# Where the root mean squares of the last three batches are made in a three-stage fp32 kernel, and when its last rows are stored and its out-projection weights split

## The chip, the core and the metric

The kernel runs on one core of a Trainium2 chip. Its time is device microseconds of one execution on that core; the time before is the median of three runs. Five engines with queues of their own do the work: TensorE (PE in the profile, with its weight loads shown as PEld), VectorE (DVE), ScalarE (ACT), GpSimd (POOL) and SyncE (SP), which here only issues DMA transfers. An engine takes its instructions in order: one that waits holds everything behind it.

## The reference

Sixteen batches of 512 rows by 512 columns pass through three layers, all in fp32. The first is a cross attention with 16 heads over 77 context rows, with a residual sum and a layer norm. The second is a mamba block: a root mean square norm of the rows, an input projection to 2320 columns, a causal convolution of 4 taps, a gated state-space scan over 16 heads, a second root mean square norm and an output projection with a residual sum. The third is another cross attention. Cut to what matters here:

```python
# layer 0, its end: the rows x1 that the mamba block takes
resid = query + out
x = (resid - mu) * rsqrt(var + 1e-5) * gamma + beta
# mamba block
def _rms(x, w):
    return x * rsqrt(mean(x * x, axis=-1, keepdims=True) + 1e-5) * w
zxbcdt = _rms(x, norm_w) @ in_proj_w          # z, xBC, dt
dt = softplus(zxbcdt[..., -16:] + dt_bias)
xBC = silu(causal_conv(zxbcdt[..., 1024:2304]))
h = h * exp(dt * A) + (dt * xh) (x) B         # per step and head; y = h . C
u = _rms((y + D_skip * xh) * silu(z), gnorm_w)
x = x + u @ out_proj_w
# then layer 2: layer norm, cross attention, residual sum
```

The change concerns the number `rsqrt(mean(x*x) + eps)` of every row of `x1`, called r1 below.

## The kernel before

**Stages.** The kernel first makes the keys and values of both attentions (`phase_kv`), then runs `PhaseA` (first cross attention), `PhaseB` (mamba) and `PhaseC` (second cross attention), each as a software pipeline written out by hand. A product of fp32 matrices is made of three matmuls of split operands, a high part (name ending in `h`) and a low part (ending in `l`): `mm3` (L36 to L38) and `mm3_late` (L44 to L47). A split is a cast on ACT and a subtraction on POOL or DVE.

**Order.** PE, DVE, ACT and POOL run their instructions in the order of the Python code (`manual_schedule`). SP does so within the marked parts of the code, among them all units of the mamba stage; the loads that `open_out` issues stand outside of them.

**The end of PhaseA.** For each of the four row blocks m of a batch, `finish` (L483 to L489) adds the residual and takes mean and variance on DVE; after the fourth, the rows' reciprocal deviation is made (for the last batch in `rstd_split`: three DVE steps and twelve small POOL steps, the Newton steps of `newton`, L95 to L98). `norm` (L506 to L508) then scales a block on ACT and applies gamma and beta in two POOL passes. `store` (L514 to L516) writes the block to DRAM through SP and squares it on ACT into the unused tile `junk`, with the row sums kept in `ssq`. `rms`, `rms_step` and `store_rms` (L523 to L534) turn `ssq` into r1 and write it to DRAM: two small activations, five small POOL steps and a DMA. For the last two batches, 14 and 15, `ssq` is kept in SBUF (`g.ssq`) and r1 is made in the mamba stage by `last_rms` at unit 12 and stored by `store_last_rms` at unit 13.

**The seam.** `close_out` and `rest` of PhaseA run woven into the start of the mamba stage. `close_out` makes r1 of batches 12 and, in part, 13. After it come, in this order of the code, the four splits of batch 0's mamba input (`head_x`, tiles `nh` and `nl`, L942 and L943), its dt projection (`head_dt`, copy `dtr`, L953), a transpose on PE (`head_turn`), softplus on DVE (`head_steps`, which ends in `da`), and the projections of the B and C parts with their convolutions. `rest` is a generator of eight steps; units 0 and 1 of the mamba stage take one step at each of their four `next(side)` places. The steps finish, norm and store the rows of batches 14 and 15. What is left of it runs after unit 1.

**The mamba stage.** There are 128 units, eight for each batch; unit i is block (b, t) with b = i // 8 and t = i % 8 (the text calls t also k), and each block is two heads. In unit i three blocks are at work: `cur` = i is projected and convolved (`projx`, `convx`, `silux`, `projz`), `prev` = i - 1 gets its decay matrix on DVE (`decay`: two scans, L1075, and a product, L1077, on the tile `dbc`), its steps on ACT (`weigh`, tile `wu`; `steps`, tile `u`), its states (`states`, `st`) and its matmuls (`intra`, L1126, to `ps_y`; `inter`, L1133, to `ps_z`), and `prev2` = i - 2 is gated (`gate`: `yt` L1139 and `ebc` L1141 on DVE, then L1142 and L1143 on POOL) and split (`gate_split`: `gh`, squares `sq` or `sqa` on ACT, `gl` and a sum on POOL). SP issues in a unit the loads of two weight blocks (`wb`, L848), of `dbc` for the current block (L1036) and of `ebc` for the previous block (L1043). From unit 6 on, half an output projection of an earlier block runs in each unit (`out_half`); `tail_norm`, `tail_pre` and `tail_end` finish a batch's output rows in the units k = 2 to 5 of the next batch.

**The next batch's input.** Beside this, units k = 0 to 5 bring batch b + 1 into shape. At k = 0 `load_x1` loads its rows to `XN` (`xn`, four DMAs, L902) and its r1 to `RS` (four DMAs, L903). `prepare` is called at one place of the units k = 1 to 5, after `intra`: at k = 1 row blocks 0 and 1 are scaled by r1 on ACT (`scale_x1`, L908); at k = 2 blocks 2 and 3 are scaled and blocks 0 and 1 turned on DVE (`turn_x1`, L126); at k = 3 blocks 2 and 3 are turned; at k = 4 the turned rows are stored (`x1t`, L919), at k = 5 loaded again (`xf`, L925).

**The out-projection weights.** `open_out` returns a generator of eight splits. Each scales a slice `xr` by the gate norm's weight (ACT, L170), casts the high part (ACT, L171), subtracts the low part (`wopl`, POOL, L172) and has SP load the slice three further on into the same buffers (L165). Units 3 to 9 take one of them each, unit 4 two, at the first `next(side)` of the unit, which stands after `convx` and before `steps`.

Of the kernel before, what the change touches and what calls it, by code (L numbers as in the profile page):

```python
# [8 lines left out]
F32 = mybir.dt.float32  # L9
FR = mybir.dt.float32r  # L10
U8 = mybir.dt.uint8
AF = mybir.ActivationFunctionType
# [280 lines left out]


class PhaseA:

# [183 lines left out]
    def finish(self, b, m):  # L480
# [9 lines left out]
        if m == KT - 1:  # L490
            rs = self.rstd(b, mv[:, :, 1], "a")
            nb_ = neg_mean(g, self.pf, mv[:, :, 0], rs, [P, KT], "nb")
            late = b - (g.nb - 2)
            self.MV[b] = (rs, nb_, g.ssq[:, late, :] if late >= 0 else self.pf.tile([P, KT], F32, name="ssq"))
            self.NP = [(b, k) for k in range(KT)]
# [14 lines left out]
    def store(self, b, m):  # L510
        g, nc = self.g, self.nc
        ssq = self.MV[b][2]
        xb = self.XB.pop((b, m))
        nc.sync.dma_start(g.x1[b][m * P:(m + 1) * P, :], xb)  # L514
        junk = self.pf.tile([P, D], F32, name="junk", bufs=1)
        nc.scalar.activation(junk, xb, AF.Square, accum_out=ssq[:, m:m + 1])  # L516
# [138 lines left out]
    def close_out(self):  # L655
# [7 lines left out]
        while self.SQ:  # L663
            self.store_next()
        self.rms(x - 1)

    def rest(self):
# [10 lines left out]
        self.norm_next()  # L678
        self.store_next()
        yield  # L680
        self.norm_next()
        self.store_next()
        yield
        for _ in range(4):
            self.store_next()
            self.norm_next()
            yield
        self.store_next()
        self.store_next()

# [60 lines left out]
class PhaseB:  # L751


    def __init__(self, g):
        self.g, self.nc = g, g.nc
        self.n = 8 * g.nb
        self.drain = False
# [16 lines left out]
    def open_out(self):  # L774
# [19 lines left out]
        return splits()  # L794

    def last_rms(self):

        y = rstd_split(self.g, self.p2, self.g.ssq.rearrange("p b k -> p (b k)"), [P, 2 * KT], "q", 1.0 / D)
        self.r_last = y.rearrange("p (b k) -> p b k", b=2)

    def store_last_rms(self):
        for j in range(2):
            self.nc.sync.dma_start(self.g.r1[self.g.nb - 2 + j], self.r_last[:, j, :])

# [90 lines left out]
    def load_x1(self, b):  # L895
# [3 lines left out]
        src = self.g.x1[b].rearrange("(a m r) d -> a r m d", m=KT, r=32)  # L899
        rs = self.g.r1[b].rearrange("(m r) a -> a r m", r=32)  # L900
        for a in range(4):
            self.nc.sync.dma_start(self.XN[32 * a:32 * a + 32], src[a])  # L902
            self.nc.sync.dma_start(self.RS[32 * a:32 * a + 32], rs[a])  # L903

# [22 lines left out]
    def prepare(self, b, step):  # L927

        if step in (1, 2):
            self.scale_x1((0, 1) if step == 1 else (2, 3))  # L930
        if step in (2, 3):
# [261 lines left out]
    def unit(self, i, side=iter(())):  # L1193
# [356 lines left out]
def tile_kernel(ctx: ExitStack, tc, ins, out, phases="kabc", dbg=None):  # L1550
# [27 lines left out]
    g.eps = cst.tile([P, 1], F32, name="eps")  # L1578
    g.ssq = cst.tile([P, 2, KT], F32, name="ssq") if "a" in phases else None
# [3 lines left out]
    A, B, C = PhaseA(g) if "a" in phases else None, PhaseB(g), PhaseC(g)  # L1583

# [32 lines left out]
    if "b" in phases:  # L1617
        B.open_main()
        with tc.manual_schedule(engines={E.SP}):
# [110 lines left out]
```

## Time and profile before

| | |
|---|---|
| median of 3 runs | 2948.78 us (2946.47 to 2951.47) |
| the profiled execution | 2947.86 us, of which 2946.1 us are the span from the first to the last instruction |
| PE busy | 2865.4 us (97%) |
| DVE, ACT, POOL busy | 2369.4 (80%), 1824.1 (62%), 1491.4 us (51%) |
| mean granted clock of PE | 0.986 |
| PE busy up to 660 us (keys, values, first attention) | 648.81 of 660.00 us |
| PE busy from 660 to 735 us | 64.23 of 75.00 us |
| PE busy from 735 to 2370 us (mamba) | 1607.87 of 1635.00 us |
| PE busy from 2370 to 2946 us (second attention) | 544.51 of 576.00 us |

A line of the timeline reads: start and length in us, engine, line of the kernel, operation, output and inputs by the program's tile names, shapes, count, and in brackets the idle time of that engine just before and what ended it. Tiles of several buffers share one name. "SPq" rows are DMA issues; their length is what SP spends on them, waiting included. A busy share is an average over stages with different limits, so what a part is worth has to be read in its own stretch of time.

### The profile page before, as it was taken

Reading aid. Unit: us, or ns where it says so; the run is one execution under the profiler, and the core shown is the slowest. Engines: PE = TensorE matmul, PEld = TensorE weight load, DVE = VectorE, ACT = ScalarE, POOL = GpSimd, SP = SyncE. Lnnn points to the kernel's source line nnn. Section 1 sums busy time; section 2 is a strip of 40 time slices with the busy share of each in tenths; the row PEclk is TensorE's granted clock in tenths of the full one; section 3 lists DMA queues with packets and bytes.
Section 4 is the critical chain, followed back from the end, with each engine's and each line's share of the span. In section 5 each row is a group of like instructions: output and inputs, shape, how many; then the busy total and the mean of one; then the engine's idle time right before and its main releaser. Section 6 shows DMA issues by size and latency. Waiting matters only on the chain.

```text
span 2946.1 us, 47590 instructions
## 1 busy us (share of the span) xinstructions
PE 2865.4 (97%) x15712; PEld 2151.8 (73%) x15712; DVE 2369.4 (80%) x3781; ACT 1824.1 (62%) x4972; POOL 1491.4 (51%) x1201
## 2 busy tenths in 40 slices
PE   9999999998899999999999999999999978999999
PEld 7755555555677888788788878878887866777776
DVE  4277777777688998998899899889989978777764
ACT  3256666665666566666666666666666547666663
POOL 1036776766756555555555555555555533333331
PEclk9999999999899999999999999999999988999999
DMA  7345665555656665665666566566656567898974
GB/s 234 95 124 157 179 180 158 162 154 170 206 181 205 206 203 183 208 215 183 203 206 207 183 207 213 183 202 206 208 186 199 170 203 214 267 270 268 272 237 147
DMA packets 421604, 578.22 MB, mean 196 GB/s; under 512 B 105982, under 2 KB 248494, under 8 KB 421358
## 3 DMA queue, kind: packets, MB, share of 16 engines
q1 hardware_dynamic: 421358, 575.18, 63.0%
q8 instruction: 125, 2.05, 0.3%
q14 instruction: 121, 0.99, 0.1%
HBM read 445.10 MB, written 129.42 MB: 195 GB/s over the span
## 4 chain that ended last, share of the span: by engine, by line
PE 69%; DVE 24%; DMA 2%; ACT 2%; issue 1%; POOL 1%; SPq 0%; DVEq 0%; ACTq 0%; POOLq 0%
PE ps_o L36 7%; PE ps_o L38 6%; PE ps_o L37 6%; PE ps_w L44 5%; PE ps_w L45 5%; PE ps_w L47 5%; DVE dbc L1075 5%; DVE acc L869 4%; DVE dbc L1077 3%; PE ps_z L1133 3%; PE ps_y L1126 2%; PE ps_y L36 2%; PE ps_s L390 2%; PE ps_z L1477 2%; PE ps_w L1433 2%; PE ps_x L417 2%
## 5 line engine op out<-in xcount | busy, mean ns | idle before, releaser
L44 PE MATMUL ps_w<-nh,wb 128*128 128x512 f32 x1092 | 454.3, 416 | 0.0
L45 PE MATMUL ps_w<-nh,wb 128*128 128x512 f32 x1092 | 430.0, 394 | 0.0
L1142 POOL TENSOR_TENSOR yt<-yt,ebc 128x384 f32<-128x384 f32 x128 | 224.1, 1751 | 396.6 <-DVE ebc L1141 396.6
L1075 DVE TENSOR_TENSOR_SCAN dbc<-dbc,delta 128x512 f32<-128x512 f32 x256 | 387.2, 1555 | 0.0
L869 DVE SCALAR_TENSOR_TENSOR acc<-ps_w,cw,acc 128x511 f32<-128x511 f32 (+2 forms) x384 | 286.1, 745 | 27.4 <-ACT acc L867 18.3
L47 PE MATMUL ps_w<-nl,wb 128*128 128x512 f32 x1092 | 293.6, 391 | 0.0
L1077 DVE TENSOR_TENSOR dbc<-dbc,gm 128x1024 f32<-128x1024 f32 x128 | 270.1, 2110 | 5.5
L1149 POOL TENSOR_TENSOR gl<-yt,gh 128x512 fp32r<-128x512 f32 x128 | 169.7, 1326 | 200.3 <-ACT gh L1148 200.2
L1143 POOL TENSOR_TENSOR yt<-yt,sz 128x512 f32<-128x512 f32 x128 | 253.9, 1984 | 10.0
L47 PEld LDWEIGHTS ps_w<-nl,wb 128*128 128x128 f32 x1092 | 205.3, 188 | 44.5
L44 PEld LDWEIGHTS ps_w<-nh,wb 128*128 128x128 f32 x1092 | 207.3, 190 | 38.5 <-issue 2.4
L45 PEld LDWEIGHTS ps_w<-nh,wb 128*128 128x128 f32 x1092 | 207.5, 190 | 35.9
L1449 POOL TENSOR_TENSOR sc<-sc,sm 128x616 f32<-128x616 f32 x64 | 78.7, 1230 | 298.3 <-DVE sm L1448 255.6
L1103 ACT ACTIVATE u<-ps_x,dt 128x64 f32<-128x64 f32 x1024 | 222.8, 333 | 0.0
L392 DVE TENSOR_TENSOR sc<-ps_s,mt 77x2048 f32<-77x2048 f32 x64 | 146.1, 2283 | 94.0 <-PE ps_s L390 93.9
L1094 ACT ACTIVATE wu<-ps_x,et 128x64 f32<-128x64 f32 x768 | 171.8, 326 | 59.8 <-PE ps_x L1085 59.8
L867 ACT ACTIVATE acc<-ps_w,cb,cw 128x512 f32<-128x512 f32 x128 | 99.8, 780 | 172.2 <-PE ps_w L47 172.2
L38 PE MATMUL ps_o<-woph,gl 128*128 128x512 f32 x496 | 196.4, 396 | 0.0
L37 PE MATMUL ps_o<-wopl,gh 128*128 128x512 f32 x496 | 196.1, 395 | 0.0
L36 PE MATMUL ps_o<-woph,gh 128*128 128x512 f32 x496 | 195.9, 395 | 0.0
L1444 ACT ACTIVATE sc<-sc,mx 128x77 f32<-128x77 f32 x512 | 176.9, 354 | 0.2 <-DVE mx L1437 0.2
L1058 ACT ACTIVATE xs<-acc 128x512 f32<-128x512 f32 x128 | 81.2, 635 | 134.2 <-DVE acc L869 128.1
(348 smaller groups left out, 7510.4 us busy)
## 6 DMA issues: line engine op xcount, KB each, us to landing
wb<-win SPq DMA_DIRECT2D x288, 512.0 KB
dbc<-dec SPq DMA_DIRECT2D x128, 512.0 KB
ebc<-ecs SPq DMA_DIRECT2D x256, 96.0 KB
pt<-pb SPq DMA_DIRECT2D x62, 384.0 KB
xt<-in_xT_dram SPq DMA_DIRECT2D x64, 256.0 KB
xb<-in_x_dram SPq DMA_DIRECT2D x64, 256.0 KB
x<-xb SPq DMA_DIRECT2D x64, 256.0 KB
xf<-x1t SPq DMA_DIRECT2D x16, 1024.0 KB
```

The lines of the kernel that those rows point to most:

```text
L36: nc.tensor.matmul(ps, ah, bh, start=start, stop=False)
L37: nc.tensor.matmul(ps, ah, bl, start=False, stop=False)
L38: nc.tensor.matmul(ps, al, bh, start=False, stop=stop)
L44: nc.tensor.matmul(ps, ah, bh, start=k == 0, stop=False)
L45: nc.tensor.matmul(ps, al, bh, start=False, stop=False)
L47: nc.tensor.matmul(ps, ah, bl, start=False, stop=k == len(rhs) - 1)
L869: nc.vector.scalar_tensor_tensor(acc[:, s:], ps[:, :S - s], cw[:, j, 3 - s:4 - s], acc[:, s:], op0=ALU.mult, op1=ALU.add)
L1075: nc.vector.tensor_tensor_scan(flat, flat, self.delta.rearrange("p c i -> p (c i)"), 0.0, op0=ALU.mult, op1=ALU.add)
L1077: nc.vector.tensor_mul(lm, lm, o.gm[:, None, :, :].to_broadcast((P, 2, 4, P)))
L1103: nc.scalar.activation(w.u[:, c, h, :], w.pu[:, f:f + 64], AF.Copy, scale=o.dtc[:, c, 2 * t + h:2 * t + h + 1])
L1142: nc.gpsimd.tensor_add(yt[:, P:], yt[:, P:], t2)
L1143: nc.gpsimd.tensor_mul(yt, yt, w.sz)
```

## The change

For the last three batches (13, 14 and 15, `own_rms`), PhaseA no longer squares the rows it stores, and neither `rms` for batch 13 nor the step at units 12 and 13 for batches 14 and 15 is there any more. The mamba stage makes r1 of these batches from the rows that it has loaded: `prepare` squares all four row blocks at k = 1 (`rms_x1`, into the tile `sq` that `gate_split` uses too) and makes r1 with `rstd_split`; at k = 2 it scales all four blocks. Their r1 is neither stored nor loaded. In `rest`, the stores come later and in groups: two at step 4, two at step 7, four after the last step, where there was one a step from step 3 to step 8 and two after it. The norms stay where they were. A unit's weight split moves from the first `next(side)` to the third, behind `load_ecs` and `head_bt` and before `intra`; the second split of unit 4 moves from the second to the fourth.

```diff
+def own_rms(g, b):
+    return b >= max(g.nb - 3, 1)
 class PhaseA:
     def finish(self, b, m):
...
-            late = b - (g.nb - 2)
-            self.MV[b] = (rs, nb_, g.ssq[:, late, :] if late >= 0 else self.pf.tile([P, KT], F32, name="ssq"))
+            self.MV[b] = (rs, nb_, None if own_rms(g, b) else self.pf.tile([P, KT], F32, name="ssq"))
     def store(self, b, m):
...
         nc.sync.dma_start(g.x1[b][m * P:(m + 1) * P, :], xb)
+        if ssq is None:
+            return
         junk = self.pf.tile([P, D], F32, name="junk", bufs=1)
         nc.scalar.activation(junk, xb, AF.Square, accum_out=ssq[:, m:m + 1])
     def close_out(self):
...
         while self.SQ:
             self.store_next()
-        self.rms(x - 1)
     def rest(self):
...
         self.finish(y, 3)
         self.norm_next()
-        self.store_next()
         yield
         self.norm_next()
         self.store_next()
+        self.store_next()
         yield
-        for _ in range(4):
+        for k in range(4):
+            self.norm_next()
+            if k == 2:
+                self.store_next()
+                self.store_next()
+            yield
+        while self.SQ:
             self.store_next()
-            self.norm_next()
-            yield
-        self.store_next()
-        self.store_next()
 class PhaseB:
-    def last_rms(self): ...
-    def store_last_rms(self): ...
     def load_x1(self, b):
...
+        self.own = self.own_rms and own_rms(self.g, b)
         for a in range(4):
             self.nc.sync.dma_start(self.XN[32 * a:32 * a + 32], src[a])
-            self.nc.sync.dma_start(self.RS[32 * a:32 * a + 32], rs[a])
+            if not self.own:
+                self.nc.sync.dma_start(self.RS[32 * a:32 * a + 32], rs[a])
+    def rms_x1(self):
+        g, nc = self.g, self.nc
+        ssq = self.p2.tile([P, KT], F32, name="ssq", bufs=1)
+        for m in range(KT):
+            junk = self.p2.tile([P, S], F32, name="sq", bufs=1)
+            nc.scalar.activation(junk, self.XN[:, m, :], AF.Square, accum_out=ssq[:, m:m + 1])
+        self.RS = rstd_split(g, self.p2, ssq, [P, KT], "q", 1.0 / D)
     def prepare(self, b, step):
-        if step in (1, 2):
-            self.scale_x1((0, 1) if step == 1 else (2, 3))
+        if step == 1 and self.own:
+            self.rms_x1()
+        elif step in (1, 2):
+            self.scale_x1(range(4) if self.own else (0, 1) if step == 1 else (2, 3))
     def unit(self, i, side=iter(())):
...
-        if self.g.ssq is not None and i == 12:
-            self.last_rms()
-        if self.g.ssq is not None and i == 13:
-            self.store_last_rms()
 def tile_kernel(ctx: ExitStack, tc, ins, out, phases="kabc", dbg=None):
...
             B.head_dt(0)
             if A:
-                A.rms_step(y - 2)
-                A.store_rms(y - 2)
                 A.project(y, 1)
                 A.finish(y - 1, 3)
...
-                B.unit(i, islice(wo, 0 if i < 3 or i > 9 else 1 + (i == 4)))
+                B.unit(i, chain((None, None), islice(wo, 0 if i < 3 or i > 9 else 1 + (i == 4))))
```

More of the change, by code (lines that the diff above doesn't have):

```diff
@@ L751, with __init__ @@
 class PhaseB:
-    def __init__(self, g):
+    def __init__(self, g, own):
         self.g, self.nc = g, g.nc
+        self.own_rms = own
         self.n = 8 * g.nb
@@ L794, in open_out @@
         return splits()
[L796 to L803, printed above, removed]
     def setup(self):
@@ L1578, in tile_kernel @@
     g.eps = cst.tile([P, 1], F32, name="eps")
-    g.ssq = cst.tile([P, 2, KT], F32, name="ssq") if "a" in phases else None
     E = mybir.EngineType
@@ L1582, in tile_kernel @@
     nc.scalar.preload_act_table_set("natural_log_exp_and_others")
-    A, B, C = PhaseA(g) if "a" in phases else None, PhaseB(g), PhaseC(g)
+    A, B, C = PhaseA(g) if "a" in phases else None, PhaseB(g, "a" in phases), PhaseC(g)
     def consts():
```

## The prediction

> **What bounds the kernel now.** I read the page's engine rows first, then ten-microsecond windows around the seam between the cross-attention stage and the mamba stage, then the timeline of each engine there, and last the timeline of one settled mamba batch.
>
> ```profile
> PE 2865.4 (97%) x15712; PEld 2151.8 (73%) x15712; DVE 2369.4 (80%) x3781; ACT 1824.1 (62%) x4972; POOL 1491.4 (51%) x1201
> ```
>
> ```profile
> 730.00:740.00 10.00, 3.57 (x23) 2.70 (x21) 2.17 (x6) 5.23 (x17) 9.17 (x15) 0.78 0.27 97
> 740.00:750.00 10.00, 5.01 (x21) 4.08 (x20) 7.53 (x6) 4.87 (x11) 9.76 (x6) 0.84 0.33 124
> ...
> 770.00:780.00 10.00, 7.79 (x52) 6.35 (x51) 8.44 (x9) 7.50 (x23) 6.56 (x5) 1.00 0.45 172
> 780.00:790.00 10.00, 9.44 (x39) 7.88 (x37) 5.71 (x10) 4.55 (x12) 6.20 (x5) 0.66 0.86 235
> ```
>
> PE is 97% busy, so only the other 3% or work on its path can move the end. The window rows give length, then busy time of PE, PEld, DVE, ACT and POOL, then granted clock, DMA share and GB/s. At the seam (730 to 830) PE is idle for 22.8 us; in the rows above it is busy for 3.57, 5.01, 7.79 and 9.44 us of 10, and the clock falls to 0.66. Who holds PE there:
>
> ```profile
> 734.77 0.63 ACT L516 ACTIVATE junk<-xb 128x512 f32<-128x512 f32 x1 [6.65 <-POOL xb L508]
> 739.92 10.65 SPq L514 DMA_DIRECT2D x<-xb  x4
> 767.83 0.33 SPq L165 DMA_DIRECT2D xr<-in_L_out_proj_w_dram  x1
> 768.69 1.09 SPq L1043 DMA_DIRECT2D ebc<-ecs  x2
> 773.00 0.56 DVE L1141 TENSOR_TENSOR ebc<-ps_z,ebc 128x384 f32<-128x384 f32 x1 [1.50 <-DMA ebc<-ecs]
> 786.63 0.56 DVE L1141 TENSOR_TENSOR ebc<-ps_z,ebc 128x384 f32<-128x384 f32 x1 [4.25 <-DMA ebc<-ecs]
> 798.78 0.56 DVE L1141 TENSOR_TENSOR ebc<-ps_z,ebc 128x384 f32<-128x384 f32 x1 [2.76 <-DMA ebc<-ecs]
> 811.65 0.56 DVE L1141 TENSOR_TENSOR ebc<-ps_z,ebc 128x384 f32<-128x384 f32 x1 [3.47 <-DMA ebc<-ecs]
> ```
>
> Two queues block at their head. ACT's squares of the last rows (L516) wait for POOL's norm of those rows (L508). SP's reload of `xr` (L165) waits until POOL's split at 765.54 (2.26 us) has read the old one, and the `ebc` load of the same unit stands behind it; DVE then waits 1.50, 4.25, 2.76 and 3.47 us for it.
>
> In a settled batch (one lasts 103 us) the chain lies on PE, but from unit k=2 to k=4 on DVE without a gap:
>
> ```profile
> 1987.69 0.60 ACT L1068 ACTIVATE sz<-ps_w 128x512 f32<-128x512 f32 x1 [0.68 <-PE ps_w L47]
> 1988.18 1.32 ACT L908 ACTIVATE xn<-xn,r 128x512 f32<-128x512 f32 x2
> 1988.82 0.75 DVE L1139 SCALAR_TENSOR_TENSOR yt<-xs,dsk,ps_y 128x512 f32<-128x512 f32 x1 [1.77 <-PE ps_y L1126]
> 1990.06 3.11 DVE L1075 TENSOR_TENSOR_SCAN dbc<-dbc,delta 128x512 f32<-128x512 f32 x2
> 2001.27 1.30 DVE L126 STREAM_TRANSPOSE xb<-xn 128x512 f32<-128x512 f32 x2
> ```
>
> From 1988.82 DVE is never idle until 2045.8, and at 2023.4 PE itself waits about 0.5 us for DVE's states. What delays DVE at 1988.82 comes out at the end one for one. That is where the change puts its new work.
>
> **What it takes away at the seam.** Durations are of one profiled execution: 2946.1 us of span, 2947.86 in all, 0.92 below the median 2948.78.
>
> Twelve squares with their reads leave ACT (0.61 us each by the steps 723.70, 724.31), with their waits on POOL. For batch 13, the squares at 696.33 and 698.95 and the two small activations at 699.71 go; now they hold ACT's four casts `nh` at 700.15 and the copy `dtr` at 702.22. PE waits 1.54 us for that copy and 0.68 us for `da` after it, 2.2 us together. The copy can then follow its matmul (697.26, 1.06 us). DVE's softplus, now from 705.77, can start 3.9 us sooner, though POOL's `nl` lies beside it and may stretch it by 1 to 2 us. The next limit is the projection of (0,0), 2.2 us sooner, and its bias on ACT, so DVE's conv moves from 718.15 to about 715.1, and POOL's Newton steps for batch 15 from 725.80 to about 722.8. I take 2.5 us, with 0 and 3.1 as ends.
>
> From there POOL's chain stays: twelve Newton steps, then the norms of six row blocks, up to 750.2. It only moves with its start, to 747.7. The last four stores still stand in SP in front of unit 2's loads (the 10.65 us row), so putting stores later doesn't free SP by itself; it lets the first `ebc` load (738.22 now) go 13 us sooner. ACT's steps `u` (736.10) come by 733 and PE runs ahead, but the gate of (0,1) needs its `ebc`, issued behind those stores. It lands at 758.4 in place of 760.93. The idle time that the squares cost (5.70 and 6.43 us on PE) mostly turns into a wait for this load; I count 2.5 us and no more.
>
> **The weight splits later.** Each is two ACT steps (0.71, 0.62), one POOL subtraction (2.26, beside DVE's scans) and one SP load. It moves past ACT's `u`, `st`, `gh`, `xs` and `sz`, past POOL's `gl` and `sqa` adds, and past SP's weight and `ebc` loads of the unit. So `ebc` of a unit goes out right after the load before it, 5 to 14 us ahead of its use. Behind the waiting `xr` load stand now the row stores `x1t` of unit 4, `xf` of unit 5 and the next unit's `dbc`. The out-projection first needs splits 0 to 3 in unit 6 and 4 to 7 in unit 10; both come in time.
>
> What is next is DVE's own work: `yt` 0.66, `ebc` 0.47, scans 3.14, product 2.05, conv 2.25, states 0.77, together 9.34 us a unit (1.2 more in unit 3 for two turns); PE needs 8.6. The scans of (0,2) to (0,6) start now at 761.41, 773.47, 787.11, 799.26 and 812.13. I expect 758.9; 769.5 (10.6 later); 778.9 (9.4 later); then, since `dbc` and `ebc` stand behind two `xr` loads of unit 4 that wait for POOL until about 781, 790.3; then PE decides with the first half out-projection in unit 6: from the states at 787.1, 0.87 + 0.44 + 2.8 + 2.8 + 0.67 + 2.8 + 1.02 + 0.87 = 12.3, and 0.47 for `ebc`, 799.9. That is 12.2 us sooner than 812.13, and nothing after that depends on the seam. Ends: 7 if the start brings nothing and the late `dbc` isn't absorbed (9.7 - 2.5); 15 if all four `ebc` waits go (12.0) with 3.1 of start.
>
> **What it adds, three times.** In unit k=1 of batches 12, 13 and 14, ACT's two scalings are replaced by four squares. They start at 1988.4 (the scratch `sq` is free when POOL's add of 1987.06, 1.30 us, is done); 4 x 0.61 plus the last read is 1991.0. Three small DVE steps (0.2 each, as `q` below) wait for them, and behind those in DVE's order stands the gate of unit k=2: `yt` goes from 1988.82 to 1991.6, +2.75. ACT itself has room: its next `wu` is wanted at 1995.4. POOL then does twelve Newton steps. The trace has that sequence once, in the part that the change removes:
>
> ```profile
> 892.31 0.16 DVE L106 TENSOR_SCALAR q_ve<-ssq 128x8 f32<-128x8 f32 x1
> 894.58 2.33 DVE L1075 TENSOR_TENSOR_SCAN dbc<-dbc,delta 128x512 f32<-128x512 f32 x2
> 896.94 1.22 DVE L1077 TENSOR_TENSOR dbc<-dbc,gm 128x1024 f32<-128x1024 f32 x1
> 892.97 0.20 POOL L95 TENSOR_TENSOR q_t<-q_y 128x8 f32<-128x8 f32 x1 [1.83 <-DVE q_y L109]
> 899.04 1.02 POOL L1142 TENSOR_TENSOR yt<-yt,ebc 128x384 f32<-128x384 f32 x1
> ```
>
> While POOL does small steps in place of its 128x384 and 128x512 ones, DVE's scans take 2.33 in place of 3.11 and the product 1.22 in place of 2.13: from `yt` to conv 4.63 us, not 6.43. So DVE gets 1.8 back and is 0.95 late. But POOL's gate is late: from the first Newton step to its end took 8.46 us, so from 1991.65 to 2000.1; ACT's `gh` (1996.40 now) follows at 2000.4, then `sqa`, `xs`, `sz`, and only then the scalings, all four now in unit k=2. The first is done at 2003.2, the second at 2003.8. DVE's turns would start at 2002.2, and wait: `yt` of unit k=3 starts at 2005.1, not 2003.12. That is 2.0 us a batch, 6.0 in all. Low end 0.95 (no wait of the turns), 2.9 in all. High end 2.75 + 1.0 without the faster scans, and the clock.
>
> On the clock: PE's idle 2.21 us before 779.02 was followed by half-speed matmuls (0.63 in place of 0.39 each), 2.4 us lost up to 787.7. My stalls in a late batch come in pieces of 0.5 and 1.5 us, and pieces of 1.37 and 0.89 us (before 792.63 and 795.03) left the clock at 1.00; so I add nothing, and 2.4 a batch at the high end, (2.75 + 1.0 + 2.4) x 3 = 18.5. [...]
>
> The rest costs nothing I can find: twelve `r1` loads (0.43 us of SP each) and three `r1` stores go, from stretches where SP waits anyway; the old last-rows step ran when DVE had just left the chain (PE's from 891.40).
>
> **The sum.** 2947.86 - 12.2 + 6.0 = 2941.7; against the median, 2942.6, 0.21% faster. A measurement of this kernel can tell about 0.2%, 5.9 us, from no change.
>
> **Rivals.** *Cheap batches*: the turns don't wait, 2.9 in place of 6.0 (for it: the once-seen sequence; against it: POOL's 8.46 us are measured): 2939.5, down to 2936 with 15 us of gain. Chance 0.15. *The block moves on*: SP's wait for `xr` now holds `x1t`, `xf` and `dbc`, and the seam gives only 7: 2947.6; for it that all loads share one queue, against it that `dbc` has a unit of lead. Chance 0.23. *Slower*: DVE's wait for the squares at k=1 with full scans and the clock loss behind it. It decides from 12.2 / 3 = 4.1 us a batch; at 6.15 it gives 2948.78 - 12.2 + 18.5 = 2955. For it: DVE has no gap from k=2 to k=4; against it: the scan of 2.33. Chance 0.12. The forecast, 2939.5 to 2946.5, keeps 0.50.
>
> Faster by over 0.2% (below 2942.9): 0.15 and some 0.31 of the forecast, 0.46. Within: the rest of the forecast and the moved block, 0.42. Slower: 0.12. The range 2936 to 2951 leaves out the slower case and little more.
>
> **What would show it.** Right: no ACT wait on POOL's `xb` at the seam; DVE's `ebc` waits gone from unit 3 on but one of several us at about 758; scans there 9 to 11 us apart; in the three late batches a DVE wait for ACT of about 4 us before the small steps, scans of 2.33, turns waiting for ACT about 1 us, and batches of about 105 us. Wrong: late batches of 103 or over 107, or `ebc` waits at 780 to 812 as before.

## The result and the profile after

The changed kernel takes 2957.03 us (median of 8 runs, 2952.98 to 2961.79), the kernel before 2950.32 (8 runs, 2946.47 to 2952.21). The ratio is 1.0023, with a 95% interval of 1.0013 to 1.0032: slower by 0.23%, where the prediction had 0.21% faster and a range that ended at 2951. The profiled execution of the changed kernel took 2961.79 us (span 2960.0), 4.8 above its median; that of before took 2947.86, 2.5 below its own. So the profiles overstate the difference, and where a time is compared below, it is a median; where a place is compared, it is an offset inside a trace.

The first row of the page, busy time by engine, shows no engine with more work:

```profile
PE 2866.9 (97%) x15712; PEld 2149.2 (73%) x15712; DVE 2372.1 (80%) x3787; ACT 1820.4 (61%) x4970; POOL 1494.9 (51%) x1220
```

The windows of the seam in the changed kernel (length; busy time of PE, PEld, DVE, ACT, POOL; granted clock, DMA share, GB/s):

```profile
730.00:740.00 10.00, 7.38 (x46) 6.20 (x47) 6.01 (x9) 8.89 (x26) 9.47 (x11) 1.00 0.31 110
740.00:750.00 10.00, 4.96 (x34) 3.54 (x32) 7.62 (x12) 1.73 (x9) 9.76 (x7) 0.94 0.21 79
750.00:760.00 10.00, 6.79 (x23) 5.70 (x24) 0.00 (x0) 5.22 (x13) 2.64 (x3) 0.55 0.98 304
760.00:770.00 10.00, 4.58 (x29) 3.52 (x27) 7.66 (x7) 3.09 (x12) 6.32 (x4) 0.80 0.43 156
...
790.00:800.00 10.00, 8.67 (x56) 7.02 (x51) 3.01 (x8) 7.43 (x22) 5.38 (x5) 1.00 0.92 258
800.00:810.00 10.00, 4.48 (x29) 3.67 (x29) 7.33 (x7) 1.61 (x4) 6.00 (x4) 0.84 0.93 319
```

PE is better off from 730 to 740 (7.38 us busy, 3.57 before), as forecast. Then two new holes stand where DVE does nothing: all of 750 to 760, and most of 790 to 800. From 730 to 830 PE is busy for 75.05 us; before it was 77.17. The timeline of the engines in the changed kernel names the holes:

```profile
733.68 15.83 SPq L518 DMA_DIRECT2D x<-xb  x6
751.48 0.62 ACT L1160 CAST gh<-yt 128x512 fp32r<-128x512 f32 x1 [9.75 <-POOL yt L1155]
753.06 1.09 SPq L1055 DMA_DIRECT2D ebc<-ecs  x2
762.24 0.56 DVE L1153 TENSOR_TENSOR ebc<-ps_z,ebc 128x384 f32<-128x384 f32 x1 [14.51 <-DMA ebc<-ecs]
783.92 4.42 POOL L172 TENSOR_TENSOR wopl<-xr,woph 128x512 fp32r<-128x512 f32 x2 [2.42 <-ACT woph L171]
786.20 0.34 SPq L165 DMA_DIRECT2D xr<-in_L_out_proj_w_dram  x1
786.64 3.55 SPq L929 DMA_DIRECT2D x1t<-xb  x4
790.29 1.28 SPq L165 DMA_DIRECT2D xr<-in_L_out_proj_w_dram  x1
793.78 1.24 SPq L1055 DMA_DIRECT2D ebc<-ecs  x2
802.56 0.56 DVE L1153 TENSOR_TENSOR ebc<-ps_z,ebc 128x384 f32<-128x384 f32 x1 [9.48 <-DMA ebc<-ecs]
```

Of the four waits of before, those for `ebc` of (0,2), (0,3) and (0,5) (1.50, 4.25 and 3.47 us) are gone or below 0.7 us, as forecast. But there is one of 14.51 us for the load of (0,1), which is issued behind the last six stores and lands 8.1 us after that, and the one for (0,4) has grown from 2.76 to 9.48 us: SP stands at unit 4's first `xr` reload until POOL has done the split, then issues four `x1t` stores, the second `xr`, weights and `dbc`, and only then `ebc`.

A late batch (the first, batch 12, from the end of unit k=1):

```profile
1990.58 0.63 ACT L912 ACTIVATE sq<-xn 128x512 f32<-128x512 f32 x1
1993.60 0.17 DVE L106 TENSOR_SCALAR q_ve<-ssq 128x4 f32<-128x4 f32 x1 [4.39 <-ACT sq L912]
1994.09 0.75 DVE L1151 SCALAR_TENSOR_TENSOR yt<-xs,dsk,ps_y 128x512 f32<-128x512 f32 x1
1995.22 2.33 DVE L1087 TENSOR_TENSOR_SCAN dbc<-dbc,delta 128x512 f32<-128x512 f32 x2
1997.58 1.22 DVE L1089 TENSOR_TENSOR dbc<-dbc,gm 128x1024 f32<-128x1024 f32 x1
2001.90 0.71 DVE L66 TENSOR_SCALAR g_y<-g_ve 128x4 int32<-128x4 int32 x1
2002.62 0.62 ACT L1160 CAST gh<-yt 128x512 fp32r<-128x512 f32 x1 [3.92 <-POOL yt L1155]
2003.44 1.16 DVE L71 SCALAR_TENSOR_TENSOR g_t<-g_y 128x4 f32<-128x4 f32 x1
2004.67 2.55 ACT L918 ACTIVATE xn<-xn,q_y 128x512 f32<-128x512 f32 x4
2006.29 1.30 DVE L126 STREAM_TRANSPOSE xb<-xn 128x512 f32<-128x512 f32 x2
```

The wait of DVE for the squares (4.39 us), the fast scans (2.33) and the product (1.22) are there as told. New are small steps of `tail_norm` that take 0.71 and 1.16 us. Before, the same two took 0.17 and 0.16 us:

```profile
1998.43 0.17 DVE L66 TENSOR_SCALAR g_y<-g_ve 128x4 int32<-128x4 int32 x1
1999.42 0.16 DVE L71 SCALAR_TENSOR_TENSOR g_t<-g_y 128x4 f32<-128x4 f32 x1
```

**A ruler.** Whole runs of the changed kernel lie up to 8.8 us apart. Inside a trace, the start of DVE's product with `gm` in each of the 128 units is far steadier: from batch 2 to batch 11 its offset against before moves by 0.6 us at most (e12_lead, which changes these batches, apart). I use these offsets for every kernel; (b,t) is the product of tile t of batch b. For the seam, the kernel's offset at the last scores of the first attention (near 670 us in all) is taken off. Columns: `dtv` of batch 0 (a tile of DVE's softplus, the start of the seam), then units, then what the three late batches add each, and the rest of the program after the mamba stage (this one from spans given to 0.1 us; all in us against before, minus is earlier):

```
kernel              dtv   (0,1)  (0,2)  (0,4)  (0,5)  (1,1) | a late batch       | after it
after             -1.56   -4.73   2.81  -1.45   5.26   3.17 | 2.81  2.77  2.92   |  3.16
splits moved only  0.59    0.56   1.08  -3.88   2.65   0.63 | none               | -0.37
splits not moved  -4.01   -7.09  -0.88  -0.60  -0.34  -0.34 | 2.80  2.78  2.88   |  0.76
ebc early         -3.63   -6.71  -6.98 -11.70  -9.60 -10.89 | 2.80  2.83  2.87   |  3.49
4 raw buffers     -1.54   -4.74   1.39  -3.54  -3.50  -5.90 | 2.83  2.77  2.91   |  0.76
before, ebc early -0.06   -1.35  -1.86  -6.87  -8.36 -10.61 | none               | -3.61
```

The seam of the changed kernel, at unit (1,1), is 3.17 us later than before in its own profile; three later kernels with the same seam code had 1.37, -2.12 and 1.13. Their mean is 0.9, where the forecast had -12.2. A late batch costs 2.8 to 2.9 us in every trace that has the change's order of steps.

### The profile page after: what moved, and what is told of

It reads as the page before. It is cut to its first block, busy times and chain, and to the rows that moved or that the text cites. A ratio compares the mean times of both kernels' runs of the same rounds, so it can differ in the third digit from the quotient of the medians.

```text
span 2960.0 us, 47593 instructions
## 1 busy us (share of the span) xinstructions
PE 2866.9 (97%) x15712; PEld 2149.2 (73%) x15712; DVE 2372.1 (80%) x3787; ACT 1820.4 (61%) x4970; POOL 1494.9 (51%) x1220
## 4 chain that ended last, share of the span: by engine, by line
PE 69%; DVE 24%; DMA 2%; ACT 2%; issue 2%; POOL 2%; SPq 0%; DVEq 0%; ACTq 0%; POOLq 0%
PE ps_o L36 7%; PE ps_o L38 6%; PE ps_o L37 6%; PE ps_w L44 5%; PE ps_w L45 5%; PE ps_w L47 5%; DVE dbc L1087 4%; DVE acc L868 4%; DVE dbc L1089 3%; PE ps_z L1145 3%; PE ps_y L1138 2%; PE ps_y L36 2%; PE ps_s L395 2%; PE ps_z L1485 2%; PE ps_w L1441 2%; PE ps_x L422 2%
## 5 line engine op out<-in xcount | busy, mean ns | idle before, releaser
L38 PE MATMUL ps_o<-woph,gl 128*128 128x512 f32 x496 | 196.0, 395 | 0.0
```

The lines of the kernel that those rows point to most:

```text
L38: nc.tensor.matmul(ps, al, bh, start=False, stop=stop)
```

## The experiments

Theory Q: the seam's gain was made and then eaten by two `ebc` loads that stand behind a blocked head of SP's queue, and a late batch costs what DVE waits for the squares. Its rivals are named in each expectation. Each ratio is to runs of the kernel before on the same chip in the same session; the interval is 95%.

### The parts: e2_rows and e1_splits

The changed kernel with the splits back at their old place:

```diff
-B.unit(i, chain((None, None), islice(wo, 0 if i < 3 or i > 9 else 1 + (i == 4))))
+B.unit(i, islice(wo, 0 if i < 3 or i > 9 else 1 + (i == 4)))
```

> The changed kernel with the weight splits back at the first and second place of the unit: the other two parts of the change alone. Theory Q: the late batches cost 2.8 us each as in the changed kernel (8.5 in all); at the seam the start is 1 us earlier and the waits of before for ebc (4.25, 2.76, 3.47 us) come back, so that (1,1) stands -2 to +1 us against before; total 2957 to 2960. Rival S: the late batches are as dear, but the seam alone is worse than before by over 2 us (the last six stores held back too long), total 2961 or more. Rival P: without the split move (1,1) stands at -3 or better, total 2952 to 2955.

2956.96 us, ratio 1.0022 (1.0012 to 1.0032). The late batches cost 2.80, 2.78 and 2.88. At the seam `ebc` of (0,1) is waited for by 13.18 us, and the waits of before come back as 1.99, 4.08, 3.02 and 2.98; (1,1) is at -0.34. As theory Q had it: rows and stores without the splits bring nothing at the seam either. (The expectations of e1_splits, e2_rows and e3_ecs count (1,1) with the attention's offset left in: so counted it is -0.06, -3.96 and -14.50. For e2_rows that is rival P's figure, but 3.6 us of it were there before the seam began, and the total lies at Q's 2957 and not in P's 2952 to 2955.)

The kernel before, with the opposite edit (that line of the change alone):

> The kernel before with one edit of the change: the weight splits of units 3 to 9 at the third and fourth place of the unit. Theory Q (the seam's gain was eaten by two late ebc loads on SP's queue: that of (0,1) behind the last row stores, that of (0,4) behind two weight reloads and the x1t stores): the waits 1.50, 4.25 and 2.76 us of before shrink below 1 us, and one wait of 6 to 10 us at (0,4) takes their place; the product of (1,1) stands 0 to +3 us against before, total 2950 to 2954. Rival S (the splits moved later are free and give what was forecast, some 9 to 10 us; the loss lies in the rows): no wait at (0,4), (1,1) at -7 or better, total 2941 to 2944. Rival P (the splits, 4.4 us of POOL in a unit, now stand before the gate and cost by themselves): (1,1) at +4 or more.

2949.23 us, ratio 0.9993 (0.9984 to 1.0002): no difference that the runs can tell. The timeline of DVE in this kernel:

```profile
742.38 0.56 DVE L1141 TENSOR_TENSOR ebc<-ps_z,ebc 128x384 f32<-128x384 f32 x1 [1.68 <-DMA ebc<-ecs]
761.30 0.56 DVE L1141 TENSOR_TENSOR ebc<-ps_z,ebc 128x384 f32<-128x384 f32 x1 [2.88 <-DMA ebc<-ecs]
800.76 0.56 DVE L1141 TENSOR_TENSOR ebc<-ps_z,ebc 128x384 f32<-128x384 f32 x1 [9.30 <-DMA ebc<-ecs]
```

These are for (0,0), (0,1) and (0,4). The waits of 1.50, 4.25 and 3.47 us of before are gone, and DVE is 3.88 us ahead at (0,4); the wait of 9.30 us for `ebc` of (0,4), 2.76 before, takes that away. So this wait is made by the moved splits alone, and rival S falls. The total is a little below the 2950 to 2954 that Q gave; the offset of (1,1), 0.63, is inside its 0 to 3.

### What blocks the queue: e3_ecs, e6_raw4, e7_ecs_old

The changed kernel with every `ebc` load one unit earlier:

```diff
 def load_ecs(self, b, t):
-    w.ebc = self.p2.tile([P, 3, P], F32, name="ebc")
+    w.ebc = self.p2.tile([P, 3, P], F32, name="ebc", bufs=3)
...
             if i:
                 self.load_decay(*cur)
+            self.load_ecs(*cur)
...
         if prev:
-            self.load_ecs(*prev)
+            pass
```

> The changed kernel, with every ebc load issued one unit earlier (with the dbc load of its unit, in a third buffer), so that no ebc load stands behind the last stores or the double reload just before its use. Theory Q: the waits of 14.5 us (0,1) and 9.5 us (0,4) for ebc go; what is next at (0,2) is its dbc load behind the stores, about 7 us earlier than the scan of 762.71; (1,1) moves from +1.7 to -6 to -9 us against before, total 2946 to 2950. Rival D (the loads are late because the DMA engines carry the stores, x1t and the weights, whatever the order of the queue): the waits stay above 4 us each, (1,1) at -2 to +2, total 2955 to 2958. Rival P (POOL with its norms and splits holds the gate, ACT waits for it): the ebc waits go but the scans hardly move, (1,1) at -3 to 0.

2945.39 us, ratio 0.9982 (0.9973 to 0.9991), against 1.0023 for the changed kernel. Its seam is 10.89 us earlier than before, close to the 12.2 of the forecast. The two longest waits left on DVE there are both for `dbc`:

```profile
751.23 2.67 DVE L1087 TENSOR_TENSOR_SCAN dbc<-dbc,delta 128x512 f32<-128x512 f32 x2 [7.13 <-DMA dbc<-dec]
786.81 2.34 DVE L1087 TENSOR_TENSOR_SCAN dbc<-dbc,delta 128x512 f32<-128x512 f32 x2 [5.62 <-DMA dbc<-dec]
```

The `ebc` waits are gone with the same transfers, which come denser (209 GB/s from 730 to 830 us, 176 in the changed kernel); rival D in its strong form falls. The seam's offset is better than the -6 to -9 expected; it started 3.63 us ahead, the changed kernel 1.56.

The changed kernel with one more raw buffer, so that an `xr` reload waits for the split before its own:

```diff
-pieces = [split_piece(g, *self.wo, k, g.i["L1_out_proj_w"], (self.o2, "xr", 3), self.gw, nc.gpsimd)
+pieces = [split_piece(g, *self.wo, k, g.i["L1_out_proj_w"], (self.o2, "xr", 4), self.gw, nc.gpsimd)
...
-        o.xr[m] = self.o2.tile([P, D], F32, name="xr", bufs=3)
+        o.xr[m] = self.o2.tile([P, D], F32, name="xr", bufs=4)
```

> The changed kernel with a fourth raw buffer for the out-projection weights, so that SP's reload after a split waits for the split before it and not for its own. Theory Q (SP stands at the xr reload of unit 4 until POOL has done the split, and holds the x1t stores and everything behind them 9 us): x1t goes out near 777 in place of 786.6, the wait of 9.5 us for ebc(0,4) falls below 2 us, (1,1) moves 5 to 8 us ahead of where the changed kernel has it, total 2949 to 2952. Rival D (ebc(0,4) is late by the DMA traffic of x1t, xf and the weights): its wait stays above 5 us, gain under 2 us.

2949.11 us, ratio 1.0003 (0.9994 to 1.0012). SP's queue and DVE at unit 4:

```profile
774.02 0.54 SPq L165 DMA_DIRECT2D xr<-in_L_out_proj_w_dram  x1
774.64 3.88 SPq L929 DMA_DIRECT2D x1t<-xb  x4
783.65 1.09 SPq L1055 DMA_DIRECT2D ebc<-ecs  x2
791.31 0.56 DVE L1153 TENSOR_TENSOR ebc<-ps_z,ebc 128x384 f32<-128x384 f32 x1 [2.63 <-DMA ebc<-ecs]
```

`x1t` goes out 12 us sooner (774.64, 786.64 in the changed kernel), `ebc` 10 us sooner (2.3 us of both were there at the end of the attention), and the wait falls from 9.48 to 2.63 us. So it was the place behind POOL's split, and not the traffic, that made most of this wait; the load still lands 6.6 us after its issue, and no run shows what part of that is traffic, or tried another engine's queue. (1,1) moved by 9.1 us against the changed kernel's own profile and by 7.0 against the nearest kernel with the same start (1.13).

The kernel before, none of the change, with the `ebc` edit of e3_ecs:

> The kernel before, none of the change, but with every ebc load issued one unit earlier in a third buffer. Theory Q (what bounds the seam is the ebc load behind SP's blocked head, not the place of the splits or the squares): the waits 1.50, 4.25, 2.76 and 3.47 us go, dbc waits of 1 to 5 us come in one or two units, (1,1) stands -6 to -10 us against before, total 2942 to 2946. Rival B (dbc, in the same queue behind the same reload, takes the place of ebc): (1,1) at -3 to 0, total 2949 to 2952.

2935.88 us, ratio 0.9957 (0.9945 to 0.9970), better than the 2942 to 2946 expected: the offset of (1,1) is -10.61, just past the -6 to -10 given, and 3.6 us more come after the mamba stage, where nothing was changed. This is the clearest answer at the seam: 10.6 us without any part of the change, 10.9 with all of it, a difference that two traces cannot tell (the changed seam alone gave 1.13 to 3.17 from the same start). e3_ecs starts 3.6 us ahead of e7_ecs_old and ends level with it. Its two `dbc` waits lie between: these loads stand behind the six grouped stores and behind the reload of the later split, and in e7_ecs_old, without the change, the longest wait for `dbc` is 0.92 us.

### What a late batch pays for: e4_small, e5_mid, e9_best

All three leave the squares of the late batches where the change put them and move what follows. e4_small, on the changed kernel:

```diff
 def rms_x1(self):
...
-        self.RS = rstd_split(g, self.p2, ssq, [P, KT], "q", 1.0 / D)
+        self.SSQ = ssq
+
+    def rms_steps(self):
+        self.RS = rstd_split(self.g, self.p2, self.SSQ, [P, KT], "q", 1.0 / D)
...
 def prepare(self, b, step):
         if step == 1 and self.own:
             self.rms_x1()
+        elif step == 2 and self.own:
+            self.rms_steps()
+        elif step == 3 and self.own:
+            self.scale_x1(range(4))
         elif step in (1, 2):
-            self.scale_x1(range(4) if self.own else (0, 1) if step == 1 else (2, 3))
-        if step in (2, 3):
+            self.scale_x1((0, 1) if step == 1 else (2, 3))
+        if step == 4 and self.own:
+            for m in range(4):
+                self.turn_x1(m)
+        if step in (2, 3) and not self.own:
```

> The changed kernel, with the steps of the late batches spread: squares at the end of unit k=1 as now, the small DVE steps and POOL's Newton steps at the end of unit k=2 (behind the gate), the four scalings at k=3, the four turns at k=4. Theory Q (the price is DVE's wait of 4.4 us for the squares and the POOL gate held by the Newton steps): a late batch costs 0.3 to 0.9 us in place of 2.85; the last product of batch 14 stands 6 to 7.5 us earlier than in the changed kernel, total 2949 to 2952. Rival N (the added work itself is the price: 2.4 us of squares on ACT, 5 us of small steps on POOL): 2 us or more a batch stay, total 2955 or more. Rival X (the later turns make x1t and xf late, and the first projection of the next batch waits): a new wait at k=0, total 2957 or more.

2960.81 us, ratio 1.0038 (1.0024 to 1.0052): slower than the changed kernel, though the wait for the squares is gone. The timeline of DVE shows why:

```profile
1987.64 0.75 DVE L1162 SCALAR_TENSOR_TENSOR yt<-xs,dsk,ps_y 128x512 f32<-128x512 f32 x1 [1.76 <-PE ps_y L1149]
2000.10 0.16 DVE L106 TENSOR_SCALAR q_ve<-ssq 128x4 f32<-128x4 f32 x1
...
2039.29 0.56 DVE L1164 TENSOR_TENSOR ebc<-ps_z,ebc 128x384 f32<-128x384 f32 x1 [3.54 <-DMA ebc<-ecs]
```

`yt` follows PE as before, `q_ve` waits for nobody, and the offset runs from -1.17 at (12,0) to -1.18, -2.66 and -3.67 at (12,1), (12,2) and (12,3). So four squares on ACT and twelve Newton steps on POOL cost nothing up to there; in the changed kernel it was the place of the small steps that cost. Then it turns: 2.26 us are lost up to (12,4), where the four turns now stand on DVE, and 3.63 up to (12,5). The `x1t` stores went out at 2023.74 (2017.83 before), and the `ebc` load of (12,4) stands behind them: a wait of 3.54 us that before did not have. Rival X was right that the later turns cost a load its lead, but the load was `ebc`, not `xf`, and its wait stood in the same batch. The three batches cost 3.45, 4.89 and 6.26 us.

e5_mid has the small steps and Newton in the middle of unit k=2 (after `tail_norm`), the scalings at the end of k=2, the turns at k=3, the stores where before had them:

```diff
         if k == 2 and i >= 10:
             self.tail_norm(i // 8 - 1)
+        if k == 2 and more and self.own:
+            self.rms_steps()
...
 def prepare(self, b, step):
...
+        elif step == 2 and self.own:
+            self.scale_x1(range(4))
...
+        if step == 3 and self.own:
+            for m in range(4):
+                self.turn_x1(m)
```

> The changed kernel, with the small steps of the late batches half a unit later and x1t where it was: squares at the end of unit k=1 as now; the small DVE steps and POOL's Newton steps in the middle of unit k=2, behind the gate and tail_norm; four scalings at the end of k=2, four turns at the end of k=3, the x1t stores at k=4 as before. Theory Q (the price of a late batch is DVE's wait for the squares, and what lengthened the last spread version was the later x1t stores): 0 to 1 us a batch in place of 2.85, total 2949 to 2952. Rival N (the added work is the price): 2 us or more a batch stay, total 2955 to 2958. Rival T (DVE's turns now wait for ACT's scalings behind the Newton steps): a new wait of 1 to 3 us at k=3.

2959.24 us, ratio 1.0040 (1.0027 to 1.0052). Theory Q's 0 to 1 us was wrong again, rival T right in kind but too low: the batches cost 4.45, 4.79 and 4.52. ACT and DVE in this kernel:

```profile
2002.15 2.56 ACT L922 ACTIVATE xn<-xn,q_y 128x512 f32<-128x512 f32 x4 [7.30 <-POOL q_y L98]
2006.62 2.32 DVE L868 SCALAR_TENSOR_TENSOR acc<-ps_w,cw,acc 128x511 f32<-128x511 f32 x3 [5.13 <-ACT acc L866]
```

ACT's scalings wait 7.30 us for POOL's Newton steps at the head of ACT's queue; behind them stands the bias `acc` of unit 3, and DVE's convolution waits 5.13 us for that. From (12,2) to (12,3) the batch loses 5.96 us; in e4_small the Newton steps stood half a unit later and the scalings a unit later, and up to (12,3) nothing was lost.

e9_best puts e4_small's order on the seam of e8_best (below), with `ebc` and `dbc` loaded a unit early:

> The version of e8_best, with the late batches as in e4_small (Newton steps at the end of k=2, scalings at k=3, turns at k=4) in place of those of e5_mid. Theory Q (e5_mid lost 6 us a batch where DVE's turns waited at k=3, e4_small 3.6 us where ebc of k=4 stood behind the later x1t; with ebc loaded a unit earlier neither is left): a late batch costs -0.5 to +0.5 us, the seam stays at 17 us, total 2928 to 2933. Rival X (xf itself, or dbc, comes late by the later x1t): 2 to 4 us a batch stay, total 2936 to 2942.

2928.46 us, ratio 0.9927 (0.9914 to 0.9939). The late batches cost -0.52, -0.49 and -0.41 us: root mean squares made from the stage's own rows can be free. The 2.8 us of the change were their order of steps, but the order of e4_small is free only with the loads a unit early: without that it cost 3.45 to 6.26 us, and e5_mid's order costs 4.5 to 4.7 with the early loads too (e8_best, next).

### The rest of the seam: e8_best, e10_old_rows, e12_lead

e8_best, on the changed kernel: the edits of e3_ecs and e5_mid, and

```diff
-            if i:
+            if i and k == 0:
                 self.load_decay(*cur)
+            if k < 7:
+                self.load_decay(cur[0], cur[1] + 1)
...
-        w.lm = self.p2.tile([P, 2, 4, P], F32, name="dbc")
+        w.lm = self.p2.tile([P, 2, 4, P], F32, name="dbc", bufs=3)
...
-        if prev2:
+        if prev2 and i == 3:
+            self.gate_split(0, 0)
+        if prev2 and i > 2:
             self.gate_split(*prev2)
...
         for k in range(4):
             self.norm_next()
-            if k == 2:
-                self.store_next()
-                self.store_next()
             yield
```

> The changed kernel with ebc one unit earlier, dbc one unit earlier too (a third buffer), the last six row stores behind those loads, the cast and split of the first gated tile one unit later (so that ACT does not wait for POOL's norms in front of xs), and the late batches as in e5_mid. Theory Q: the remaining waits at the seam (7.1 and 5.6 us for dbc, 6.8 us of PE for xs) go in good part: (1,1) 13 to 18 us ahead of before counted from the end of the attention stage (10.9 with ebc alone), late batches 0 to 1 us each, total 2934 to 2942. Rival P (POOL's twelve Newton steps, norms and splits bound the seam): no more than 11 to 12 us at the seam, total 2941 to 2945.

2945.41 us, ratio 0.9993 (0.9984 to 1.0001); outside both totals, as e5_mid's late batches cost 13.8 us here too (4.66, 4.47, 4.68). The seam did what Q gave, 17.6 us ahead (13 to 18), not the 11 to 12 of rival P. e9_best has 16.7, and PE is busy for 90.49 us from 730 to 830, against 77.17 before.

e10_old_rows: the kernel before with early `ebc` and `dbc` and the later cast, none of the change:

> The kernel before, none of the change, with ebc and dbc one unit earlier and the first gated tile's cast and split one unit later. Theory Q (the seam's price is in SP's order and in ACT behind POOL's norms; the change's own part at the seam is what its squares hold, 2 to 4 us at the start): (1,1) 12 to 15 us ahead of before, total 2932 to 2936. Rival E (the change's earlier start and later stores are needed for it): no better than with ebc alone, 10 to 11 us, total 2936 to 2939.

2936.54 us, ratio 0.9955 (0.9943 to 0.9968); the offset of (1,1) is -9.2, so Q's 12 to 15 was wrong and rival E right: with the squares still in their old place, more lookahead adds little to e7_ecs_old. (Its start fell 2.35 us behind before, for the clock, see below; from `dtv` on it gains 11.5, e7_ecs_old 10.6.) With both loads early the change's own part counts: 16.7 in e9_best against 9.2, of which 2.4 us are the clock at e10_old_rows' start and 4.0 the earlier start of e9_best.

e12_lead: e9_best with the rows of the batch after next loaded at the end of unit k=7, and scalings and turns one unit earlier (`prepare_early`, from batch 1 on).

```diff
-        if more and k == 0:
-            self.load_x1(more)
+        if i == 0:
+            self.load_x1(1)
...
+        if more and i >= 8 and k < 6:
+            self.prepare_early(more, k)
...
+        if k == 7 and i // 8 + 2 < nb:
+            self.load_x1(i // 8 + 2)
```

> The version of e9_best, with x1 of the batch after next loaded at the end of unit k=7 and its scalings and turns one unit earlier, from batch 1 on (own rows: squares at k=0, small steps k=1, scalings k=2, turns k=3). Theory V (a settled batch is bound by DVE from k=2 to k=4, where the turns of k=3 lie, and by PE before it): 0.5 to 1.5 us less in each of 14 batches, total 2912 to 2925. Rival U (PE takes over at once, or the earlier load is late): no change within 2 us of e9_best, or slower.

2925.65 us, ratio 0.9925 (0.9913 to 0.9938), not told apart from e9_best. Over eleven settled batches it gains 5.0 us in the trace, 0.45 each, and its late batches lose 0.55 each. Theory V's 0.5 to 1.5 was too high; what takes over from DVE there was not followed.

### A tile of 32 bytes: e11_pad

After the mamba stage the changed kernel loses 3.16 us more, in code that is the same. The offset grows evenly, from 0.17 at 104 us into that part to 2.38 at its last score step, and likewise in all kernels with the rows' change, in none without. In the first attention the same kernels gain evenly, 1.06 us in the changed one from 165 to 670 us. The change removes `g.ssq`, 32 bytes a partition in the pool of constants, so every later tile lies elsewhere.

```diff
 g.eps = cst.tile([P, 1], F32, name="eps")
+g.spare = cst.tile([P, 2, KT], F32, name="spare")
```

> The changed kernel with an unused tile of 32 bytes a partition in the pool of constants, the size of the ssq tile that the change took out, so that all later tiles lie where they lay before. Theory Z (the steady loss of some 2.3 us in the second attention, 0.04 us a score step, and the gain of 0.8 us in the first come from the 32 bytes by which the tiles moved): both drifts vanish, below 0.3 us; total 1 to 2 us below the changed kernel, 2955 to 2957. Rival W (they come from something else, or from the execution): the drift of 2 us or more stays.

2955.52 us, ratio 1.0017 (1.0008 to 1.0026). Both drifts are gone: the offset in the first attention stays at -0.56 to -0.57, that in the second at -1.32 to -1.29. Theory Z holds. The groups of PE's matmuls from 2500 to 2800 us (busy time, mean ns), the changed kernel first and then e11_pad:

```profile
L36 PE MATMUL ps_o<-wo1h,ct1h 128*128 128x512 f32 x153 | 64.6, 422 | 0.0
L37 PE MATMUL ps_o<-wo1l,ct1h 128*128 128x512 f32 x152 | 60.1, 395 | 0.0
```

```profile
L36 PE MATMUL ps_o<-wo1h,ct1h 128*128 128x512 f32 x154 | 64.6, 420 | 0.0
L37 PE MATMUL ps_o<-wo1l,ct1h 128*128 128x512 f32 x154 | 60.3, 392 | 0.0
```

e11_pad has the means of before (420 and 392). So 2 to 3 ns in two of the three matmuls of an output projection (1 in the third, L38, 394 to 395) come with the 32 bytes; which operand's place does it was not tried.

## Why the prediction was wrong, step by step

**The start (2.5 us, ends 0 to 3.1).** ACT's copy `dtr` and the softplus came sooner as told, but by one of two amounts: `dtv` is 1.5 us earlier in four traces with the change (the changed kernel among them) and 3.6 to 4.0 in the others. The granted clock decides (windows of 3 us: the changed kernel, then e2_rows, then e11_pad):

```profile
678.00:681.00 3.00, 1.31 (x12) 0.48 (x16) 2.93 (x5) 2.82 (x4) 2.92 (x4) 0.93 0.41 135
681.00:684.00 3.00, 3.00 (x16) 0.44 (x8) 3.00 (x2) 0.95 (x2) 2.92 (x4) 0.50 0.47 154
684.00:687.00 3.00, 3.00 (x11) 2.28 (x8) 2.55 (x1) 0.00 (x0) 2.92 (x3) 0.50 0.47 149
```

```profile
681.00:684.00 3.00, 3.00 (x19) 1.72 (x17) 3.00 (x2) 0.00 (x0) 2.92 (x3) 1.00 0.63 200
684.00:687.00 3.00, 2.29 (x12) 1.62 (x9) 2.93 (x6) 0.28 (x1) 2.92 (x4) 1.00 0.37 132
```

```profile
681.00:684.00 3.00, 3.00 (x20) 0.87 (x16) 3.00 (x2) 1.91 (x4) 3.00 (x3) 0.51 0.33 96
684.00:687.00 3.00, 3.00 (x11) 1.17 (x4) 3.00 (x2) 0.00 (x0) 2.92 (x3) 0.50 0.58 207
```

In the changed kernel PE is idle for 2.84 us up to 679.69 and then runs over 6 us at half clock; in e2_rows the idle time is 1.29 us and the clock stays. But the idle time does not settle it: e4_small, e6_raw4 and e11_pad, the other three with 1.5 us, were idle for only 1.30 or 1.31 us and ran over 6 us at half clock too. e10_old_rows, without the change, has 2.86 us, then 0.59 and 0.50, and its `dtv` comes 2.35 us later than in before. The term was right in kind; its size went with the clock, and no run shows what settles which of the two sizes a trace has.

**The seam (12.2 us): the step that failed, and the larger error.** The forecast saw both loads and under-priced both. The scan of (0,2) was to start at 758.9 and started at 762.71: `ebc` of (0,1) took 8.1 us to land where the step used the 5.7 of before, and the start gave POOL 1.1 us, not 2.5. (Stores, three `xr` and two weight loads go out ahead of it in both kernels; the next weight and `dbc` loads follow 1.1 to 1.3 us closer behind it in the changed one. Whether that made it slower was not tried.) The scans of (0,3) and (0,4) followed 10.4 and 10.7 us later (10.6 and 9.4 forecast): 5.0 us late in all. The step "stand behind two `xr` loads of unit 4 that wait for POOL until about 781, 790.3" broke the sum: SP was freed at 786.2, as ACT reached the splits only after `xs` (781.47) and `sz`; then came `x1t` (3.55 us) and the second `xr` (1.28) in the queue, and the load landed 7.5 us after its issue. The scan of (0,5) started at 803.03, 12.7 us late, the whole gain, and 7.7 of it from this term; e6_raw4 and e1_splits show it by taking most of that wait away and by making it alone. The rival "the block moves on" named this mechanism, with 7 us left of the gain; it too was low.

**The late batches (2.0 us each; measured 2.8).** Right: squares at 1988.4 (1990.58 less the offset of 2.16), `yt` +3.11 for +2.75, scans 2.33 and product 1.22, POOL's chain of Newton and gate 8.33 us for 8.46. The squares' pitch was 0.755 us, not 0.61: the 0.61 was the step from a square to a scaling of another tile, which started 0.09 us after the start of the square's read of its sum (724.22, 724.31 in before); a further square started 0.22 us after it (1991.11, 1991.33 in the changed kernel). Wrong: the turns were to wait for ACT's scalings; they did not (2006.29, right behind `tail_pre`), because DVE had lost 1.5 us before that in `tail_norm`, whose twelve small steps took 3.91 us in place of 2.37 (two of them, of 0.71 and 1.16 us, ended at 2002.61 and 2004.60, each 0.02 us after a POOL step on 128x512 tiles that they began beside: the gate's, 2001.31 to 2002.59, and that of `gl`, 2003.32 to 2004.58). The next `yt` came 2.9 us late for the 2.0 forecast. Of the rival "cheap batches" the condition came true, as the turns did not wait, and the price did not. The high end (6.15 with the clock) did not come either: the clock was 1.00 from 1980 to 2300 us.

**What was not in the sum.** The move of the later tiles: a gain of 1.1 us in the first attention and a loss of 2.2 in the second.

**The balance.** Mean seam 0.9, late batches 8.5, tiles 1.1: 10.5 us by the traces, which on the profiled 2947.86 of before makes 2958.4, where the median after is 2957.03. The forecast's error is 14.4 us (2957.03 against 2942.6): 13.1 for the seam, 2.5 for the late batches and 1.1 for the tiles make 16.7; 0.9 goes off, as the profile of before lay that far below the median the forecast started from, and 1.4 stays open, less than the runs scatter. The new order of the last stores was not tried by itself.

## What to carry to other kernels

A load that moves up in a queue only helps if nothing ahead of it waits for an engine (here DVE waited 9.48 us for `ebc` of (0,4) behind an `xr` reload that waited for POOL's split, and 2.63 us where that reload waited for the split before): before moving work, list for each queue the head that blocks, what releases it and what stands behind, and do not take a landing time over from another place in the queue (5.7 us before, 6.6 to 8.1 here). A load that needs no fresh data belongs a whole unit ahead of its use; here that, with one more buffer of 1.5 KB a partition, was worth 10.6 us on the kernel before. Extra work on engines with idle time can be free or cost a wait by its place: the same squares and Newton steps cost -0.5, 2.8 or 4.5 us a batch (the first with the loads early too), so put the reader of a slow result behind the critical engine's next link, not ahead of it.

## What the runs showed of the hardware

At the start of the seam, idle times of PE of 1.30 or 1.31 us (e4_small, e6_raw4, e11_pad) and of 2.84 or 2.86 us (the changed kernel, e10_old_rows) were followed by over 6 us at half clock, and 1.27 to 1.35 us at the same place (before, e2_rows, e5_mid, e7_ecs_old, e9_best, e12_lead) were not. Some 8 us earlier an idle time of 2.06 us was followed by half clock in twelve of the fourteen traces (in before 0.55 from 674 to 676 us, matmuls of 0.63 us) and left it at 1.00 in the changed kernel (matmuls of 0.39 us) and e10_old_rows. So in these traces the length of the idle time does not decide alone.

Moving all later tiles by 32 bytes a partition changed the mean of two groups of output-projection matmuls by 2 to 3 ns of 392 and 420 and, over one stage, the time by 2.2 us, where the two kernels differ by 6.7 in all. With effects of 0.2% in view, a tile that merely goes away is part of the change.
